# A gated-attention layer and a graph-attention layer on one core: the row of edge values turned on VectorE and carried through DRAM, and all step orders written anew

## The chip, the cores and the metric

The kernel runs on one core of a Trainium2 chip. The metric is the device time of one execution in microseconds (us), the median of several runs. Five engines work side by side on a core, each with its own instruction queue that it works off in order: TensorE (PE) multiplies, VectorE (DVE), ScalarE (ACT) and GpSimd (POOL) do elementwise work, and SyncE (SP) issues the DMAs. They wait for each other through semaphores.

## The reference

For each of 64 graphs with N = 256 nodes and H = 512 features there are two layers, each added to its input (`_layernorm` has no weights).

```
h = relu(layernorm(x))                                  # layer 0
q, k, v = h @ Wq.T, h @ Wk.T, h @ Wv.T                  # 8 heads of 64
attn = softmax(where(adj != 0, q k^T / 8, -inf))
c = attn @ v
gate = sigmoid(concat(c, h) @ Wg.T + bg)
x = x + gate * h + (1 - gate) * c

h = relu(layernorm(x))                                  # layer 1
Wh = h @ W
e_i, e_j = Wh @ a[:512], Wh @ a[512:]                   # one value per node each
e = leaky_relu(e_i[:, None] + e_j[None, :], 0.2)
p = softmax(where(adj == 0, -1e9, e), axis=2)
x = x + elu(p @ Wh)
```

## The kernel before

All arithmetic is fp32. The 256 nodes of a graph are two tiles of 128 partitions (`t` = 0, 1). The work on one graph is cut into some 215 named steps (`@step`, L358), each of which issues a few instructions on one engine. The text `PLAN` (L23) gives each step a number; L988 to L998 add 48 times the graph's number, sort all steps of all graphs by that sum and issue them in this order. The numbers serve for sorting only. The order on every engine is thus written out by hand, and steps of four or five graphs alternate. `MOVED` (L52) holds numbers of their own for graphs 0, 1, 2 and the last three, `ONCE` those of loading and preparing weights. `HOMES` says which of 8 PSUM banks (and which SBUF slot) a tile occupies; "5/7" means 5 for even graphs and 7 for odd ones. A tile put in a slot waits for the last reader of what was there before.

Each product with a weight (`qk`, `v`, `z` for the gate, `wh`) and `po` (attention times Wh) runs as seven half-size products instead of eight (`product`, L444). The seven accumulate in three PSUM tiles: tile a takes products 1 and 2, tile b takes 6, 7, 4, tile c takes 5, 3. Between them VectorE or ScalarE reads the intermediate states: `u1` reads a after 1; `u2` reads b after 6, `u3` reads b after 7, `c10` reads b after 4; `c11` reads c after 5, `c01` reads c after 3; `c00` reads a after 2. So product 7 may not start before `u2` has read b, product 4 not before `u3`, product 3 not before `c11`, product 2 not before `u1`. The operand sums that this needs (`Sh`, `Sg`, `Sc`, `S1`, `Sp`, `Rp`) are made on GpSimd (L442, L896, L906).

The other steps that matter below:

- `sc.0`, `sc.1` (L656): scores of four heads each, eight matmuls into four banks `ps`. `max` (L666, VectorE) adds the mask and takes the row maximum, two instructions for each head; `exp` (L676, ScalarE), `rec` (VectorE), `scale` (L692 GpSimd, L690 ScalarE), `turn` (L698, VectorE, 32x32 blocks), `send` and `fetch` (L554, L559, DMAs through DRAM that put the blocks in place), `we` (L716, attention times v), `cT` (L725, ScalarE), `tc` (L735), `sc_c` and `fc` (through DRAM again).
- `z.c10b`, `z.c11b`, `z.u2b` (L481, GpSimd): add the bias. `tanh` (L774, ScalarE). `diff` (L764, GpSimd): d = h - c. `plus` (L769, GpSimd): x = x + c. `mix` (L778, VectorE): d = (z + 1) d, for t = 0 and 1. `res` (L782, VectorE): x = x + d / 2. `st0`, `st1` (L506): statistics of the layer norm; `root` (L517, GpSimd), `nb` (L522), `nm` (L527, ScalarE), `th` (L535, VectorE), `sh` and `fh` (DMAs through DRAM).
- `ej` (L834): the row e_j. It is column HH of `wh[:, t, 1]`, one value per partition. For t = 0 and 1 TensorE transposes this column, broadcast to 128 columns, with the identity, so that the PSUM tile `pe` holds e_j along the free dimension on each partition. `lo` (L840, VectorE): logits from `pe`, e_i as a scalar for each partition, and the mask. `lk` (L847): leaky ReLU. `gm` (L851): row maximum. `gx` (L856, ScalarE): exponential and sums. `tg` (L867, VectorE), `sg` and `fg` (four DMAs each, L543 and L550): the turned matrix `egT`. Then `Sp`, `po`, `gr` (reciprocal), `neg`, `xn`, `pos`, `elu` (L951), `add` (L959, GpSimd), `store`.

With the numbers of `PLAN`, TensorE's repeating order from one graph's `sc.0` to the next one's is, with the graph in brackets, relative to that of `sc.0` (no bracket: the same graph):

```
sc.0 we.10(-1) we.11(-1) we.00(-1) we.01(-1) sc.1 v.7 v.5 z.1(-1) v.4 v.3 wh.1(-2) wh.6(-2) wh.5(-2) wh.7(-2)
wh.2(-2) v.2 wh.3(-2) wh.4(-2) ej(-2) z.6(-1) qk.1(+1) z.5(-1) z.7(-1) z.2(-1) z.4(-1) z.3(-1) qk.6(+1) qk.2(+1)
qk.7(+1) qk.5(+1) qk.4(+1) po.1(-2) v.6(+1) po.6(-2) po.5(-2) po.2(-2) po.7(-2) qk.3(+1) po.4(-2) po.3(-2) v.1(+1)
```

The part of VectorE's order around the reads of `qk`'s bank b, and of GpSimd's order beside it:

```
VectorE: ... z.c01(-1) mask(+1) qk.u2(+1) mix.0(-1) gr(-2) mix.1(-1) res.0(-1) res.1(-1) qk.u3(+1) st1.1(-1) ...
GpSimd:  ... diff.1(-1) z.c11b(-1) z.c10b(-1) diff.0(-1) plus.0(-1) plus.1(-1) Rp.1(-2) Rp.2(-2) Sh.3(+1) Sp.0(-2) ...
```

Of the kernel before, what the change touches and what calls it, by code (L numbers as in the profile page):

```python
# [8 lines left out]
F32 = mybir.dt.float32  # L9
# [14 lines left out]
load@-53.229 st0.0@-40.331 st0.1@-39.212 root0@-32.441 nb0@-32.4 nm0.0@-31.757 nm0.1@-31.065 th.0@-30.253  # L24
th.1@-29.213 sh@-20.792 edges@-19.41 fh@-16.267 Sh.2@-12.847 qk.1@-11.156 Sh.0@-7.731 Sh.1@-4.634 qk.u1@-4.111
qk.6@-2.798 qk.2@-1.025 mask@-0.706 qk.u2@-0.186 qk.7@0.517 qk.5@0.645 qk.u3@1.668 qk.4@1.724 Sh.3@2.277
qk.c00@2.902 v.6@6.373 qk.c11@6.599 qk.c10@7.236 qk.3@10.925 v.1@13.726 sc.0@13.916 max.000@14.395 v.u1@14.853
max.010@15.863 max.001@15.981 max.011@16.298 qk.c01@16.63 v.u2@17.05 exp.000@17.735 sc.1@17.987 exp.010@18.004
v.7@18.092 v.5@18.445 max.100@18.691 max.101@18.934 v.u3@19.508 v.c11@19.513 exp.011@20.27 max.110@20.373
max.111@21.033 exp.001@21.056 v.4@23.294 v.c10@23.754 v.3@23.804 exp.101@24.169 rec.01@24.371 v.c01@25.071  # L30
exp.111@25.413 rec.00@26.384 v.2@28.003 exp.110@28.347 rec.11@29.321 scale.111@29.428 scale.011@30.052
scale.110@30.582 turn.011@30.677 turn.111@31.368 scale.001@31.418 scale.010@31.434 scale.000@31.808
exp.100@32.801 v.c00@33.423 turn.110@37.208 send.11@37.78 rec.10@38.601 turn.001@39.658 scale.101@40.247
turn.010@40.875 turn.000@41.467 scale.100@41.474 send.00@43.588 turn.101@43.788 send.01@45.424 turn.100@45.566
send.10@52.665 fetch.11@55.316 fetch.00@56.632 Sg.0@61.755 fetch.10@62.154 fetch.01@62.554 Sg.1@62.628
we.10@63.137 we.11@63.14 we.00@63.143 we.01@63.146 cT.1@65.083 cT.0@65.432 Sc.2@65.47 Sg.2@65.68 z.1@68.201
Sc.0@68.336 Sc.1@71.528 tc.0@73.01 Sc.3@74.703 tc.1@74.778 Sg.3@82.424 z.6@83.522 z.u1@83.782 again.0@84.027
sc_c@84.628 fc@85.006 z.u2@85.037 z.u2b@86.195 z.5@86.868 z.7@86.934 z.u3@88.511 z.c11@88.533 z.2@89.652
z.4@91.004 again.1@92.033 z.c10@92.428 z.c00@92.667 z.3@93.14 diff.1@93.363 z.c11b@93.809 z.c10b@93.814
diff.0@93.855 plus.0@93.873 z.c01@93.901 tanh.11@94.368 plus.1@94.403 tanh.00@95.334 tanh.01@95.604 mix.0@96.297  # L40
tanh.10@96.664 mix.1@96.757 res.0@96.891 res.1@97.036 st1.1@99.721 st1.0@101.016 root1@101.658 nb1@104.063
nm1.1@105.297 nm1.0@107.607 th1.1@108.104 th1.0@108.66 sh1@111.487 fh1@113.781 S1.0@117.405 S1.1@117.725
wh.1@121.42 wh.6@121.622 S1.2@121.67 wh.5@121.818 wh.u1@122.472 wh.u2@122.877 wh.7@123.017 wh.2@123.434
wh.u3@124.432 wh.c11@124.598 wh.c00@125.372 S1.3@125.392 wh.3@126.07 wh.4@126.758 wh.c01@127.005 ej@127.191
wh.c10@127.609 lo.1@128.353 lo.0@129.336 lk@129.602 Rp.0@129.808 gm@131.759 gx.1@132.877 gx.0@133.43 tg@136.267
sg@136.289 Rp.1@144.203 gr@144.671 fg@145.239 Rp.2@145.991 Sp.0@148.311 Sp.1@148.553 po.1@148.676 at.0@148.676
at.1@148.686 Sp.2@149.761 po.6@152.304 po.u1@152.662 po.u2@152.749 Sp.3@153.211 po.5@153.801 po.2@154.345
po.7@154.622 po.u3@154.882 po.c11@155.143 Rp.3@155.395 po.4@156.259 po.c10@156.723 po.3@156.853 po.c00@156.874
neg.1@157.002 xn.1@157.023 po.c01@157.396 pos.1@159.011 elu.1@160.16 neg.0@163.197 add.1@163.978 pos.0@164.566
xn.0@164.664 elu.0@166.071 add.0@174.142 store.1@183.43 store.0@183.43  # L50
# [3 lines left out]
load@-69.188 st0.0@-50.682 st0.1@-46.872 nb0@-45.939 nm0.0@-43.244 nm0.1@-40.355 th.1@-36.948 Sh.0@-31.306  # L54
qk.1@-21.868 Sh.1@-15.043 Sh.2@-8.6 qk.6@-5.632 qk.u1@-5.223 qk.2@-3.198 edges@-2.003 qk.u2@-0.488 Sh.3@0.768
qk.7@2.104 qk.u3@3.685 qk.5@5.031 qk.4@7.534 qk.c11@8.518 qk.c10@8.614 mask@8.785 qk.3@9.496 qk.c00@9.714
qk.c01@10.925 sc.0@11.768 max.000@12.349 exp.000@12.811 max.011@13.719 max.010@13.827 v.1@13.828 exp.011@14.039
v.u1@15.075 v.6@16.297 max.001@16.537 v.u2@16.712 exp.010@16.947 sc.1@17.125 v.7@18.128 v.5@18.608
max.100@18.752 Sg.0@19.682 max.110@22.794 rec.01@22.94 exp.001@24.137 exp.110@24.623 max.111@24.962
scale.010@25.268 v.u3@25.413 exp.111@25.859 max.101@26.25 rec.00@26.894 scale.011@27.011 rec.11@28.365  # L60
turn.010@28.388 v.c11@28.435 scale.110@28.625 turn.011@30.554 scale.111@30.803 turn.110@31.058 scale.000@32.929
turn.111@37.156 v.2@37.693 send.01@37.944 exp.100@38.055 send.11@39.05 v.4@39.065 exp.101@39.254
scale.001@39.872 turn.000@40.017 Sg.2@40.1 v.c10@40.679 rec.10@40.871 turn.001@41.71 v.c00@42.426 v.3@43.287
scale.100@44.231 turn.100@44.288 send.00@44.4 scale.101@44.579 fetch.11@45.445 turn.101@47.476 send.10@47.487
v.c01@49.156 fetch.00@57.727 we.11@59.431 fetch.01@59.996 fetch.10@60.188 we.00@60.876 we.01@63.055 we.10@64.19
cT.0@65.308 cT.1@66.064 again.1@66.53 Sg.1@67.233 Sc.2@70.084 tc.1@71.129 Sc.0@71.252 Sc.1@72.531 z.1@73.791
tc.0@75.343 z.6@76.16 z.u1@76.575 z.5@78.53 sc_c@78.596 z.u2@79.103 z.7@81.738 Sg.3@82.04 Sc.3@82.269 z.2@84.937
fc@84.984 again.0@85.551 z.u3@85.933 z.4@86.156 z.c11@88.877 z.u2b@89.227 z.c11b@89.268 z.3@90.528 z.c10@90.685
z.c00@92.236 z.c10b@93.083 z.c01@93.161 diff.0@93.789 diff.1@95.348 tanh.10@95.709 plus.1@96.041 tanh.00@96.265
tanh.01@97.623 tanh.11@98.195 mix.1@100.765 plus.0@101.798 mix.0@102.293 res.1@102.32 res.0@102.484  # L70
st1.1@103.015 st1.0@103.627 root1@104.452 nb1@104.489 nm1.0@104.861 th1.0@105.045 nm1.1@105.996 th1.1@106.074
sh1@110.257 fh1@114.941 S1.0@118.51 S1.1@118.914 wh.1@119.88 wh.u1@121.045 wh.6@122.08 wh.u2@122.882
wh.5@123.346 wh.2@124.489 S1.2@124.759 S1.3@125.052 wh.7@126.446 wh.u3@127.178 wh.c11@127.993 wh.3@129.051
wh.4@129.297 wh.c01@129.526 wh.c10@129.674 ej@129.753 wh.c00@129.961 lo.1@130.044 Rp.0@130.295 lo.0@130.34
lk@130.611 Rp.1@131.752 gm@132.017 gx.0@132.213 gx.1@132.222 Rp.2@134.288 tg@134.329 sg@139.346 gr@146.73
fg@147.354 Sp.0@147.882 Sp.1@148.085 po.1@148.711 po.5@149.418 po.6@149.54 Rp.3@150.947 po.u1@151.6 Sp.2@151.822
po.u2@152.389 po.2@152.556 po.7@152.971 Sp.3@153.454 po.u3@154.535 po.4@155.138 po.c11@156.295 po.c10@156.812
po.3@157.112 po.c00@157.127 po.c01@157.915 neg.1@157.97 xn.1@157.979 neg.0@158.113 pos.0@158.418 pos.1@158.918
xn.0@159.242 elu.1@160.812 elu.0@162.404 add.0@162.854 add.1@165.627 store.1@179.067
""",  # L80
    1: """
load@-66.388 edges@-62.194 st0.0@-56.02 st0.1@-45.366 root0@-45.352 nb0@-40.605 nm0.0@-39.939 nm0.1@-39.434
th.1@-21.412 qk.1@-21.165 Sh.2@-20.499 Sh.0@-16.11 Sh.1@-16.042 qk.u1@-14.221 mask@-8.988 v.1@-8.931 qk.6@-3.549
v.6@-2.01 qk.u2@-1.609 v.u1@-0.158 qk.2@1.34 qk.7@2.079 qk.u3@2.277 qk.c00@3.165 Sh.3@3.954 qk.5@4.267
qk.4@5.138 v.u2@5.757 v.7@6.871 qk.c11@7.006 qk.3@7.543 qk.c10@8.787 v.u3@9.481 sc.0@11.208 max.000@12.204
qk.c01@12.588 max.010@13.45 exp.000@15.083 exp.010@15.517 max.011@15.659 exp.011@15.787 max.001@15.848
sc.1@15.867 exp.001@16.394 rec.01@17.779 max.101@19.324 max.110@19.389 scale.010@19.44 max.111@19.747
rec.00@20.491 v.2@21.238 max.100@22.063 exp.100@23.114 exp.110@23.868 v.5@24.004 scale.000@25.701 v.c11@25.88
scale.011@25.97 scale.001@26.999 v.4@27.999 turn.010@28.906 turn.000@29.132 v.c10@29.391 exp.111@30.212
turn.011@30.506 v.c00@30.783 rec.11@30.983 exp.101@32.076 scale.110@32.481 turn.001@33.017 v.3@33.133  # L90
rec.10@35.239 send.00@36.274 send.01@37.842 scale.100@38.531 scale.111@38.803 scale.101@39.584 fetch.00@39.916
# [194 lines left out]
def kernel(  # L286
# [13 lines left out]
    nc = tc.nc  # L300
    B, N, H = x.shape
    NH = 8
    DK = H // NH
    P = 128
# [528 lines left out]
    @step("ej")  # L833
    def edge_row(s, g):  # L834
        pe = s["pe"] = bank([P, N], "pe", g)
        for t in range(NT):
            nc.tensor.transpose(pe[:, t * P:(t + 1) * P], to_wh(s, g, t, 1)[:, HH:].to_broadcast([P, P]), ident)
# [193 lines left out]
```

## Time and profile before

| | |
|---|---|
| median of 3 runs | 3175.8 us (3175.29 to 3176.8) |
| profiled execution | 3175.03 us, of which the span from first to last instruction is 3173.2 |
| TensorE busy | 3097.0 us (98%), granted clock 0.997 |
| VectorE busy | 2607.4 us (82%) |
| GpSimd busy | 2176.8 us (69%) |
| ScalarE busy | 1506.8 us (47%) |
| DMA packets' share of 16 engines | 72.5%, 589.25 MB in the kernel's queue |
| `pe` transposes, TensorE | 128 matmuls, 24.4 us busy in all |

Busy time counts each instruction from start to end, and neighbours overlap in their pipelines; what an instruction costs a full queue is the distance from its start to the next one's. "Idle before" names whatever released the instruction last. Line numbers are those of the kernel before.

### The profile page before, as it was taken

To read this page: it belongs to the slowest core of one execution; us is meant where nothing else is said; L and a number is where in the kernel's file an instruction comes from. 1 tells how busy PE (TensorE), PEld (TensorE's weight loads), DVE (VectorE), ACT (ScalarE), POOL (GpSimd) and SP (SyncE) were. 2 spreads that over 40 slices of the span, in tenths; PEclk is the share of its full clock that TensorE was granted. 3 is DMA by queue.
4 is the path that set the end of the run, shared out by engine and by line. 5 is a ranking of instruction groups with operands and counts; after the bars stand their busy time and mean duration, and the time that the engine had idled before them with its cause. 6 is when DMAs were issued, how large, how long until landed. Compare 5 with 4: busy or idle time off the path is not lost.

```text
span 3173.2 us, 61830 instructions
## 1 busy us (share of the span) xinstructions
PE 3097.0 (98%) x19542; PEld 2673.1 (84%) x19542; DVE 2607.4 (82%) x6625; ACT 1506.8 (47%) x4165; POOL 2176.8 (69%) x3006
## 2 busy tenths in 40 slices
PE   9999999999999999999999999999999999999997
PEld 8888888888888888888888888888888888888885
DVE  8888888888888888888888888888888888888885
ACT  4445445455454454554544545445445454454452
POOL 4666676676766766767667667676676676766765
PEclk9999999999999999999999999999999999999998
DMA  8677776777777767777677777776776777777772
GB/s 236 166 201 179 190 204 172 195 196 180 198 177 191 204 169 196 198 178 200 177 191 203 172 196 198 177 201 176 191 204 171 196 196 177 203 176 194 194 175 81
DMA packets 1107157, 593.20 MB, mean 187 GB/s; under 512 B 687632, under 2 KB 1032720, under 8 KB 1106832
## 3 DMA queue, kind: packets, MB, share of 16 engines
q1 hardware_dynamic: 1106832, 589.25, 72.5%
q8 instruction: 157, 2.57, 0.3%
q14 instruction: 168, 1.38, 0.1%
HBM read 306.45 MB, written 282.59 MB: 186 GB/s over the span
## 4 chain that ended last, share of the span: by engine, by line
PE 78%; DVE 11%; issue 6%; DMA 5%; SPq 1%; POOL 0%; ACT 0%; DVEq 0%; POOLq 0%; ACTq 0%
PE pmb_z L457 8%; PE ps L656 8%; PE pc L716 7%; PE pmb_qk L457 6%; PE pma_z L457 5%; PE pmb_v L457 5%; PE pmb_wh L457 5%; PE pmc_z L457 5%; PE pmc_qk L457 4%; PE pma_qk L457 3%; PE pma_wh L457 3%; DMA there_e<-eb 3%; PE pma_v L457 3%; PE pmc_wh L457 3%; PE pmc_v L457 3%
## 5 line engine op out<-in xcount | busy, mean ns | idle before, releaser
L676 ACT ACTIVATE e<-e,low 128x256 f32<-128x256 f32 x1024 | 506.1, 497 | 8.8 <-DVE low L666 8.8
L666 DVE CUSTOM_DVE_ANT_0 e<-ps,mask 128x256 f32<-128x256 f32 x1024 | 379.6, 418 | 89.1 <-PE ps L656 88.1
L442 POOL TENSOR_TENSOR Sc<-cT 128x256 f32<-128x256 f32 x128 | 104.3, 815 | 506.0 <-ACT cT L725 506.0
L692 POOL TENSOR_SCALAR e<-e,rec 128x256 f32<-128x256 f32 x768 | 359.4, 485 | 18.6 <-DVE rec L683 15.4
L698 DVE STREAM_TRANSPOSE eb<-e 128x512 f32<-128x512 f32 x512 | 341.1, 688 | 0.5 <-POOL e L692 0.4
L774 ACT ACTIVATE z<-z 128x256 f32<-128x256 f32 x256 | 99.6, 412 | 405.9 <-POOL z L481 248.6
L527 ACT ACTIVATE h<-x,nb_l,rs_l 128x512 f32<-128x512 f32 x256 | 195.0, 808 | 183.3 <-DVE nb_l L522 75.8
L656 PE MATMUL ps<-qk 64*128 64x256 f32 x2048 | 255.7, 389 | 0.0
L656 PEld LDWEIGHTS ps<-qk 64*128 64x128 f32 x2048 | 187.9, 186 | 61.6 <-issue 23.2
L716 PE MATMUL pc<-eT,v 128*64 128x256 f32 x2048 | 236.7, 383 | 0.8 <-DMA eT<-there_e 0.8
L716 PEld LDWEIGHTS pc<-eT,v 128*64 128x64 f32 x2048 | 141.0, 137 | 87.9 <-issue 22.4
L676 ACT ACTIVATION_READ_ACCUMULATOR e<-e,low 128x1 f32 x1024 | 193.3, 189 | 0.0
L959 POOL TENSOR_TENSOR x<-x,po 128x512 f32<-128x512 f32 x126 | 160.3, 1272 | 32.1 <-DVE po L951 18.6
L476 ACT COPY u_po<-pma_po 128x256 f32<-128x256 f32 x63 | 23.4, 372 | 330.7 <-PE pma_po L457 321.6
L506 DVE BATCH_NORM_STATS2 bs_l<-x 128x6 f32<-128x512 f32 x256 | 172.9, 675 | 3.7 <-DMA x<-in_x_dram 3.6
L769 POOL TENSOR_TENSOR x<-x,c 128x512 f32<-128x512 f32 x128 | 172.2, 1363 | 1.5 <-DMA c<-there_c 1.1
L517 POOL TENSOR_TENSOR rs_l<-ve_l,mhalf 128x2 f32<-128x2 f32 (+1 forms) x129 | 90.4, 700 | 116.5 <-DVE ve_l L513 106.4
L535 DVE STREAM_TRANSPOSE h<-h 128x512 f32<-128x512 f32 x248 | 167.3, 694 | 0.3 <-ACT h L527 0.3
L764 POOL TENSOR_TENSOR d<-d,c 128x512 f32<-128x512 f32 x128 | 164.4, 1285 | 0.0
L778 DVE SCALAR_TENSOR_TENSOR d<-z,d 128x512 f32<-128x512 f32 x128 | 163.5, 1280 | 0.9 <-POOL x L769 0.6
L481 POOL TENSOR_TENSOR z<-z,bias 128x256 f32<-128x256 f32 x128 | 92.9, 727 | 97.2 <-DVE z L472 96.8
L782 DVE SCALAR_TENSOR_TENSOR x<-d,x 128x512 f32<-128x512 f32 x128 | 145.7, 1175 | 0.4
(175 smaller groups left out, 8953.5 us busy)
## 6 DMA issues: line engine op xcount, KB each, us to landing
there_e<-eb SPq DMA_DIRECT2D x256, 512.0 KB, 4.5
eT<-there_e SPq DMA_DIRECT2D x1024, 128.0 KB, 4.4
there_h<-h SPq DMA_DIRECT2D x496, 128.0 KB, 3.3
there_c<-cb SPq DMA_DIRECT2D x64, 512.0 KB, 3.5
c<-there_c SPq DMA_DIRECT2D x256, 128.0 KB, 2.9
x<-in_x_dram SPq DMA_DIRECT2D x63, 512.0 KB, 4.4
out_dram<-x SPq DMA_DIRECT2D x63, 512.0 KB, 3.7
hT<-there_h SPq DMA_DIRECT2D x248, 128.0 KB, 3.0
```

What stands on the lines that cost most here:

```text
L457: nc.tensor.matmul(s[name, key][(slice(None), *cols)], lhsT, rhs, start=first and i == 0, stop=last and i == len(mms) - 1, skip_group_chec ...
L506: nc.vector.bn_stats(bs, s["x"][:, t, :])
L527: nc.scalar.activation(out, s["x"][:, t, :], AF.Relu, bias=s["nb", layer][:, t:t + 1], scale=s["rs", layer][:, t:t + 1])
L535: nc.vector.transpose(h, h)
L656: nc.tensor.matmul(s["ps", half, jj, i][:, t, :], qk[r:r + DK, 0, jj, t * P:(t + 1) * P], qk[r:r + DK, 1, jj, :], start=True, stop=True,)
L666: nc.vector.tensor_tensor_reduce(e[:, i, t, :], s["ps", half, jj, i][:, t, :], s["mask"][:, t, :], -SCALE, HUGE, ALU.add, ALU.min, accum_o ...
L676: nc.scalar.activation(e, e, AF.Exp, bias=s["low", half][:, jj, i, t:t + 1], scale=-1.0, accum_out=sums[:, jj, i, t:t + 1])
L692: nc.gpsimd.tensor_scalar(e, e, rec, 1.0, ALU.mult, ALU.mult)
L698: nc.vector.transpose(eb[:, :, 4 * i:4 * i + 4, :].rearrange("p b n c -> p n b c"), e)
L716: nc.tensor.matmul(pc[i * DK:(i + 1) * DK, jj, :].rearrange("p (t a c) -> p t a c", t=NT, c=32), s["v"][:, kc, hd * DK:(hd + 1) * DK], s[" ...
L764: nc.gpsimd.tensor_tensor(d, d, s["c"][t], ALU.subtract)
L769: nc.gpsimd.tensor_tensor(xt, xt, s["c"][t], ALU.add)
```

## The change

Three things are changed. First, `ej`, for all graphs but the last two (g < LAST = 62): VectorE turns the column, broadcast to 16 columns for each t, as 32x32 blocks into a tile `turned`. Rows 0 and 16 of each block of 32 partitions then hold the block's 32 values. A new step `sj` sends them to DRAM (two DMAs of four runs of 128 bytes), a new step `fj` reads the 1 KB row back onto all 128 partitions of an SBUF tile from a new pool `row` of one buffer. `lo` is the same instruction and reads that tile in place of PSUM. Second, all of `PLAN`, `MOVED` and `ONCE` has new numbers, and so the order on each engine is another one. Third, `HOMES` is new: other banks and slots.

```
@@ -315,7 +321,7 @@
     const = pool("const", 1)
     st = pool("st", 4)
     kept = pool("kept", 5)
-    sb = {tag: pool(tag, bufs) for tag, bufs in {"x": 5, "mask": 3, "hT": 3, "wh": 1, "R": 1}.items()}
+    sb = {tag: pool(tag, bufs) for tag, bufs in {"x": 5, "mask": 3, "hT": 3, "wh": 1, "R": 1, "row": 1}.items()}
     large, medium = pool("large", 1), pool("medium", 1)
     ps = pool("ps", 1, space=bass.MemoryType.PSUM)
     dram = pool("dram", 4, space=bass.MemoryType.DRAM)
...
@@ -832,9 +838,27 @@
 
     @step("ej")
     def edge_row(s, g):
+        if g < LAST:
+            s["turned"] = small([P, 32], "turned", f"{g}")
+            e = s["wh"][:, :, 1, HH:].to_broadcast([P, NT, 16])
+            return nc.vector.transpose(s["turned"].rearrange("p (t k) -> p t k", t=NT), e)
         pe = s["pe"] = bank([P, N], "pe", g)
         for t in range(NT):
             nc.tensor.transpose(pe[:, t * P:(t + 1) * P], to_wh(s, g, t, 1)[:, HH:].to_broadcast([P, P]), ident)
+
+    @step("sj")
+    def send_row(s, g):
+        if g < LAST:
+            s["there_row"] = dram.tile([NT, 4, 32], F32, tag="row", name=f"there_row_{g}")
+            for t in range(NT):
+                rows_t = s["turned"].rearrange("(b r) c -> b r c", r=32)[:, 16 * t, :]
+                nc.sync.dma_start(s["there_row"][t], rows_t)
+
+    @step("fj")
+    def fetch_row(s, g):
+        if g < LAST:
+            s["pe"] = new("row", [P, N], "row", g)
+            nc.sync.dma_start(s["pe"], spread(s["there_row"].rearrange("t b c -> (t b c)"), N))
 
     @step("lo.0", "lo.1")
     def logits(s, g, t):
```

Of the two `PLAN` texts, the entries of the new one that stand around the steps named above (numbers for sorting only):

```
+edges@3.711 qk.3@3.892 qk.c01@4.382 qk.c00@4.567 mask@7.258 sc.0@8.025 max.001@8.607 max.010@10.017
+max.011@12.971 max.000@13.147 exp.001@14.657 exp.000@17.098 v.6@18 rec.00@19.203 v.1@19.938 exp.010@20.508
...
+wh.u3@127.396 S1.3@127.77 wh.2@128.093 wh.4@129.921 wh.c11@130.169 wh.3@130.313 wh.c01@131.348 ej@131.525
+wh.c00@132.014 wh.c10@133.179 sj@135.375 fj@137.689 lo.0@139.236 lo.1@139.363 lk@139.554 gm@139.674 gx.1@141.342
```

New homes of some PSUM tiles (even graphs/odd graphs):

```
pmb_po@7/5 ps_0_0_1@7/4 ps_0_1_0@5/7 ps_0_1_1@0 pmb_v@7/0 pma_po@4/2 pmc_po@1/4
```

Sorted by the new numbers, TensorE's repeating order is:

```
sc.0 po.1(-3) po.6(-3) v.6 po.5(-3) po.7(-3) po.2(-3) v.1 po.4(-3) po.3(-3) sc.1 z.1(-1) v.2 v.7 wh.1(-2) wh.6(-2)
wh.5(-2) wh.7(-2) v.5 wh.2(-2) wh.4(-2) wh.3(-2) z.6(-1) v.4 v.3 z.5(-1) z.7(-1) z.2(-1) z.4(-1) qk.1(+1) z.3(-1)
qk.6(+1) qk.5(+1) qk.7(+1) qk.2(+1) qk.4(+1) qk.3(+1) we.00 we.11 we.01 we.10
```

VectorE's, from `sc.0` on:

```
max.001 max.010 max.011 max.000 gr(-3) po.u2(-3) th.0(+1) tc.0(-1) rec.00 po.u3(-3) po.c11(-3) th.1(+1) po.c10(-3)
neg.1(-3) po.c01(-3) tc.1(-1) rec.01 neg.0(-3) max.111 elu.1(-3) v.u2 max.101 max.110 max.100 turn.001 wh.u2(-2)
elu.0(-3) wh.u3(-2) wh.c11(-2) turn.000 turn.011 turn.010 wh.c01(-2) ej(-2) v.u3 v.c11 rec.11 rec.10 wh.c10(-2)
v.c10 z.u2(-1) v.c01 turn.111 turn.110 z.u3(-1) turn.101 turn.100 z.c00(-1) z.c11(-1) st0.0(+2) z.c10(-1) lo.0(-2)
lo.1(-2) lk(-2) gm(-2) z.c01(-1) tg(-2) qk.u2(+1) st0.1(+2) mix.0(-1) mix.1(-1) qk.u3(+1) qk.c11(+1) res.1(-1)
res.0(-1) st1.1(-1) st1.0(-1) qk.c10(+1) nb1(-1) qk.c01(+1) th1.1(-1) nb0(+2) th1.0(-1) mask(+1)
```

Parts of GpSimd's (running on into the next round, with graphs still counted from this one) and SP's:

```
GpSimd: ... Sc.3(-1) z.u2b(-1) Sg.3(-1) Sh.3(+1) z.c10b(-1) z.c11b(-1) diff.1(-1) plus.1(-1) diff.0(-1) root0(+2)
        plus.0(-1) root1(-1) Rp.0(-2) Sg.2 Sg.0 Rp.1(-2) Rp.3(-2) Sp.0(-2) Sp.1(-2) Sg.1 Rp.2(-2) Sp.2(-2) ...
SP:     sh1(-2) fh1(-2) sh(+1) sc_c(-1) fh(+1) store(-3) send.00 send.01 sj(-2) load(+2) fc(-1) fj(-2) send.11
        fetch.01 send.10 fetch.00 fetch.11 sg(-2) fetch.10 edges(+1) fg(-2)
```

## The prediction

> **What bounds the kernel now.** I read the page's busy line first, then the TensorE timeline of two stretches, then the list of waits, then the chain of waits between 1539 and 1549 us, then the ranges of single VectorE instructions.
>
> ```profile
> PE 3097.0 (98%) x19542; PEld 2673.1 (84%) x19542; DVE 2607.4 (82%) x6625; ACT 1506.8 (47%) x4165; POOL 2176.8 (69%) x3006
> ```
>
> TensorE is the bound, and only about 2% of it is idle. The timeline shows that the work repeats in rounds, one graph further each time. One round starts with the scores of the first half (`sc.0`):
>
> ```profile
> 189.03 2.00 PE L656 MATMUL ps<-qk 64*128 64x256 f32 x16
> ...
> 236.86 2.00 PE L656 MATMUL ps<-qk 64*128 64x256 f32 x16
> ...
> 1507.09 2.00 PE L656 MATMUL ps<-qk 64*128 64x256 f32 x16
> ...
> 1555.95 2.00 PE L656 MATMUL ps<-qk 64*128 64x256 f32 x16
> ```
>
> The reader is to take differences of starts. Nearly every round lasts 1555.95 - 1507.09 = 48.86 us. The round from 189.03 lasts 47.83 us; in it TensorE shows no wait. So a wait of 1.03 us stands in the usual round. The list of waits names it, and the chain shows how it comes about:
>
> ```profile
> PE pmb_qk L457 <- DVE u_qk L472: 51.8, 62, 0.9
> ```
> ```profile
> 1539.34 1.80 PE pmb_qk L457 x16
> ...
> 1541.83 1.48 DVE d L778
> 1543.30 0.06 DVE rec L864
> 1543.36 1.00 issue
> 1544.36 0.14 DVE x L782
> 1544.50 1.00 issue
> 1545.49 1.21 DVE x L782
> 1546.70 0.61 DVE u_qk L472
> 1547.32 0.04 issue
> 1547.36 2.05 PE pmb_qk L457 x16
> ```
>
> `qk.4` may not add to PSUM bank b before VectorE has read it (`qk.u3`). Its operand was ready when `qk.7` ended, about 1544.6, but VectorE was inside the two `mix` and two `res` steps until 1546.70. Those are slow because they meet GpSimd:
>
> ```profile
> L778 DVE SCALAR_TENSOR_TENSOR d<-z,d x128: 677/1150/1746, 80.2 to 3136.6; 128x512 f32<-128x512 f32 x128
> L782 DVE SCALAR_TENSOR_TENSOR x<-d,x x128: 677/1209/1575, 82.0 to 3139.1; 128x512 f32<-128x512 f32 x128
> ```
>
> The same instruction takes 677 ns at best and about 1200 in the median.
>
> [...] The transfers that repeat every round here land in 2.9 to 4.5 us (medians) and are far larger[...]. [...]
>
> **The change part by part.** All sums are per round, with time 0 at `sc.0`.
>
> *Transposes removed.* In the timeline the two `pe` transposes start at 1526.81 and the next step at 1527.03: 0.22 us, wholly on TensorE's path. A round without any wait becomes 47.83 - 0.22 = 47.61 us.
>
> *Row sent instead.* `ej` on VectorE: 32 columns; reciprocals of 4 columns take 156 ns, a transpose of 512 takes 688, so 0.15 to 0.2 us. `sj` adds two DMA issues and `fj` one to SP: issues with 128 rows or blocks cost 0.43 (`eT`) to 0.8 us, so 0.9 to 2.4 us of queue, and I take 1.5. `lo` now reads two SBUF operands instead of one in PSUM: 0.48 us each now, at worst 2 x 0.5 us longer when GpSimd is met, at best a little shorter. None of this is on TensorE's path if the row lands in time. In the new order `ej` comes after `wh.c01`, about 20 us; `sj` is issued by 21.5 and lands by 24 to 26; load and four fetches (0.47 + 1.74) stand before `fj`, so SP waits at most some 2 us there; the row lands by 27 to 30. `lo` stands behind `z.c10`, whose product ends at about 30. Cost: nothing, as long as that holds; a later row would hold VectorE, and behind it `lk`, `gm`, `tg` and `qk.u2`, for which TensorE waits.
>
> *The u_qk wait.* Laying the new TensorE order end to end with the start-to-start times of the timeline (`sc` 1.93, `po` 0.43, `v` and `wh` 0.87, `z` 1.73, `qk` 1.79, `we` 0.90) puts `qk.6` at 32.9, `qk.5` 34.7, `qk.7` 36.5, `qk.2` 38.3, `qk.4` 40.05. `qk.u3` can start at 38.5 and must start by 39.3. Ahead of it on VectorE now stand only `qk.u2` (34.9 to 35.6), `st0.1` (0.8) and two `mix`; the two `res` come after it. `mix` waits for `diff.0`: GpSimd starts `z.c10b` at about 30.4, then 0.7 + 0.7 + 3 x 1.27 = 35.6. So `mix.0` starts at 36.5 and meets `plus.0` (1.2 us), `mix.1` does not (0.6): 38.3. `qk.u3` is in time with 0.8 us to spare, and the 1.03 us go.
>
> *What is late next.* At the start of the round the new order puts `po.1`, `po.6`, `v.6`, `po.5`, `po.7` right after `sc.0`, where four `we` stood. The homes give `pmb_po` of one parity the bank of `ps_0_1_0` of the other. So `po.6`, due at 2.46 (1.93 + 0.43 + 0.1 that TensorE loses when it changes from scores to other products), waits for `max.010`. In the trace the first max starts 1.16 us after `sc.0`, and each takes 0.69: `max.001` 1.16 to 1.85, `max.010` from 2.0, read by 2.8. That is 0.35 to 0.4 us. Then `po.7` needs `po.u2`, which stands behind `max.011`, `max.000` and `gr` (2.75 + 0.69 + 0.69 + 0.1 = 4.2, read by 4.6); TensorE comes there at 2.85 + 0.43 + 0.87 + 0.43 = 4.58: about even. In rounds of the other parity `v.6` needs `max.011`'s bank (3.5 against 3.3). After a wait TensorE loses another 0.1 (1.00 us instead of 0.89 for the first eight matmuls after 1547.36). Together 0.45 to 0.75 us, and I take 0.6.
>
> *Round and total.* 47.61 + 0.6 = 48.21, against 48.86: 0.65 us less. 58 rounds follow the repeating order and six have orders of their own with smaller waits of the same kind; I count 60: 39 us. The profiled execution took 3175.03 us (span 3173.2 and 1.8 around it); the median of the runs, 3175.8, is 0.8 above it. So 3175.8 - 39 = 3137. The first and last graphs are reordered too; the trace can't price that, and I allow 6 us either way.
>
> **Rivals.**
> - *No new wait*: the maxes start earlier than I think, or the banks come free. For it: TensorE now waits nearly nowhere else. Against: two maxes are 1.4 us of VectorE after scores that take 1.9. Round 47.61, 1.25 x 60 = 75 less: 3101.
> - *The old wait is replaced in full*: GpSimd runs 1 to 2 us later than laid out, `mix.0` meets more, `qk.u3` is late again, on top of the wait at `po.6`. For it: GpSimd's list is long just there. Against: 0.8 us to spare and two `res` moved away. Round 48.5 to 48.95: 3155 to 3181, and I name 3165.
> - *Slower: the second layer's chain sets the round.* `lo` to `po.1` took 1527.61 to 1549.25 = 21.6 us; in the new order 30.3 to 50.1 (`po.1` of the next round), 19.8, with an SP queue of 55 DMAs instead of 52 between. Laid out: `gm` ends 32.4, `gx` 34.0, `tg` 34.7, four sends 3.25, `fetch.10` (4 x 0.6) and `edges` 0.4 go before `fg` (3.3), last landing 4.2 after its issue: 48. TensorE's first `po.1` waits for that landing at 50.1, so 2.1 us are spare. A delay of the row, of `tg` or of SP beyond 2.1 + 0.65 = 2.75 us makes the kernel slower; at 3.4 us the round is 49.5 and the time 3175.8 + 0.65 x 60 = 3215. For it: SP is in order, `sg` waits for VectorE, and landings of `eT` reach 6.6 us. Against: three independent steps would have to slip.
>
> That the change doesn't do what it says is possible only for the spreading apart: one of four `mix` and `res` still meets GpSimd in my layout, which the sum contains.
>
> **How the numbers follow.** Forecast 3137 (its own range 3120 to 3153): 0.52. No new wait: 0.17. Old wait replaced in full: 0.20, of which a third lies within 0.2% (6.4 us, about what can be told from no change here). Slower chain: 0.11. Faster by over 0.2%: 0.52 + 0.17 + 0.14 = 0.83; within: 0.06; slower: 0.11. The range from 3094 to 3176 leaves out the slower chain, the top of the third case and the bottom of the second.
>
> **What would show it.** Right: `pe` gone from TensorE; the wait of `pmb_qk` for `u_qk` near 0; new waits of 0.3 to 0.5 us of `pmb_po` (and `pmb_v` in every second round) for the max steps; `mix` and `res` with medians under 0.9 us except one; a round of 48.1 to 48.4. Wrong: `pma_po` waiting for the landing of `egT`, `eg` (`lo`) waiting for the row's DMA, a `pc` wait for `eT`, or `pmb_qk` still waiting about 1 us. Any wait at another step of TensorE above 0.3 us a round breaks the sum.

## The result, and the profile after

The changed kernel takes 3173.3 us (median of 12 runs, 3167.5 to 3182.5), the kernel before 3176.9 (12 runs on the same chip, 3175.3 to 3178.0). The ratio is 0.9989, with a 95% interval of 0.998 to 0.9999. The forecast was 3137. So 3.6 us were gained where 39 were expected. Also the runs now lie 15 us apart where they lay 3 us apart. The profiled execution of the changed kernel took 3169.5 us (span 3167.6, clock 0.997).

The busy line of the changed kernel:

```profile
PE 3106.2 (98%) x19418; PEld 2656.4 (84%) x19418; DVE 2579.7 (81%) x6687; ACT 1484.6 (47%) x4165; POOL 2182.6 (69%) x3006
```

TensorE has 124 matmuls fewer (62 graphs of two transposes), yet it is as full as before. The waits of TensorE over the whole span (what was waited for; total us, times, longest):

```profile
PE pmb_po L463 <- POOL Sp L920: 20.0, 57, 2.8
PE pmb_qk L463 <- DVE u_qk L478: 9.9, 13, 2.7
PE pc L722 <- DVE qk L478: 4.4, 28, 0.2
PE pc L722 <- DMA eT<-there_e: 4.3, 2, 2.7
```

The wait of 51.8 us in 62 pieces for `u_qk` is gone except for 13 pieces. Two groups are new, one in nearly every round (`pmb_po`) and one in every second round (`pc`). The ranges of `mix` and `res` (minimum, median, maximum in ns) are now those of undisturbed instructions:

```profile
L784 DVE SCALAR_TENSOR_TENSOR d<-z,d x128: 650/691/1759, 78.4 to 3131.5; 128x512 f32<-128x512 f32 x128
```
```profile
L788 DVE SCALAR_TENSOR_TENSOR x<-d,x x128: 659/684/1302, 80.7 to 3133.2; 128x512 f32<-128x512 f32 x128
```

They had medians of 1150 and 1209. So both things that the change is made of did happen. The timeline of TensorE shows where the rest went. It holds the starts of three rounds and the steps around the new waits (start, duration, step; in brackets the idle time and what ended it):

```profile
1503.40 2.00 PE L662 MATMUL ps<-qk 64*128 64x256 f32 x16
...
1506.35 0.67 PE L463 MATMUL pmb_po<-Rp,Sp 128*128 128x256 f32 x2 [0.24 <-POOL Sp L920]
1506.95 1.13 PE L463 MATMUL pmb_v<-wv_t,Sh 128*128 128x256 f32 x4
1507.91 0.59 PE L463 MATMUL pmc_po<-wh,Sp 128*128 128x256 f32 x2
...
1548.17 1.08 PE L722 MATMUL pc<-eT,v 128*64 128x256 f32 x8
1549.41 2.81 PE L722 MATMUL pc<-eT,v 128*64 128x256 f32 x24 [0.16 <-DVE qk L478]
1552.15 2.00 PE L662 MATMUL ps<-qk 64*128 64x256 f32 x16
...
1555.11 0.67 PE L463 MATMUL pmb_po<-Rp,Sp 128*128 128x256 f32 x2 [0.33 <-POOL Sp L920]
1555.61 1.03 PE L463 MATMUL pmb_v<-wv_t,Sh 128*128 128x256 f32 x4
1556.47 0.59 PE L463 MATMUL pmc_po<-wh,Sp 128*128 128x256 f32 x2
...
1596.80 3.67 PE L722 MATMUL pc<-eT,v 128*64 128x256 f32 x32
1600.40 2.00 PE L662 MATMUL ps<-qk 64*128 64x256 f32 x16
```

Rounds now alternate: 1552.15 - 1503.40 = 48.75, and 1600.40 - 1552.15 = 48.25. At 1555.11 `po.6` waits 0.33, as forecast. The profile names GpSimd's `Sp` as the releaser. But the sum that `po.6` reads, `Sp.1`, had ended at 1553.2; it is `max.010`, whose second instruction ended at 1554.95, that sets the bank free. (In the last experiment below all four `Sp` of a round end before `max.010` does, and `po.6` still starts 2.95 us into the round.)

In rounds like the one from 1503.40, `v.6` has the bank of `max.011`, which ended at 1506.88: it starts at 1506.95, 0.60 after `po.6` where the other round has 0.50, and `pmc_po` comes 0.96 after it instead of 0.86. The forecast had this too; the list of waits doesn't show it, since the matmuls before it hadn't ended.

The new thing is 1549.41. The four `we` groups of an odd graph take 1552.15 - 1548.17 = 3.98 us, those of an even one 1600.40 - 1596.80 = 3.60. In between, `we.11` waits for the bank of `pc_1`, which in that parity is the bank of `pmc_qk` that `qk.c01` still reads. That is 0.38 in every second round.

A third thing happens in some rounds only. First SP's queue in one of them, then VectorE, then TensorE:

```profile
1818.20 2.02 SPq L565 DMA_DIRECT2D c<-there_c  x4
1820.35 0.35 SPq L861 DMA_DIRECT2D row<-there_row  x1
```
```profile
1826.84 2.35 DVE L866 SCALAR_TENSOR_TENSOR eg<-row,wh,mask 128x256 f32<-128x256 f32 x2 [0.84 <-DMA row<-there_row]
1829.22 1.64 DVE L872 SCALAR_TENSOR_TENSOR eg<-eg 128x512 f32<-128x512 f32 x1
```
```profile
1834.08 1.16 PE L463 MATMUL pmb_qk<-Sh,wq_t 128*128 128x128 f32 x8 [1.46 <-DVE u_qk L478]
```

The row is fetched behind four fetches of `c`, and by the start of `lo` it lands 6.5 us after its issue (1820.35 to 1826.84; the DMA packets' share in between was 1.11). `lo` waits 0.84 for it. Started late, the two `lo` and `lk` meet GpSimd's `diff` and `plus` (1827.45 to 1830.31): they take 2.35 us and 1.64; in an undisturbed round they take 1.35 and 1.10. So `gm`, `tg` and then `qk.u2` are late, and `qk.7` stands 1.46 us. That round lasts 50.48. The fetch is not a small transfer, either. It writes the 1 KB row onto 128 partitions:

```profile
row<-there_row SPq DMA_DIRECT2D x1, 128.0 KB
```

That is as much as one fetch of `eT` moves.

From the starts of the scores I worked out where the span stands against that of before:

```
stretch                              before    after    difference
to the first scores                    24.0     24.2      +0.2
first six rounds                      261.7    263.7      +2.0
the 54 repeating rounds              2639.2   2628.0     -11.1
the last rounds and the tail          248.3    251.7      +3.4
```

In the 54 rounds, 48.21 a round was forecast, 2603.3 in all. The 24.7 above it are, but for rounding, 27 x 0.38 = 10.3 at `we.11`, 8.8 in ten rounds longer than 48.25 or 48.76, and 27 x 0.04 + 27 x 0.17 = 5.7, since a round with nothing but the waits at `po.6` and `v.6` is 48.25 or 48.38 (seen below) and not 48.21.

### The profile page after: what moved, and what is told of

It is laid out like the page before. It is cut to its first block, busy times and chain, and to the rows that moved or that the text cites. A ratio compares the mean times of both kernels' runs of the same rounds, so it can differ in the third digit from the quotient of the medians.

```text
span 3167.6 us, 61736 instructions
## 1 busy us (share of the span) xinstructions
PE 3106.2 (98%) x19418; PEld 2656.4 (84%) x19418; DVE 2579.7 (81%) x6687; ACT 1484.6 (47%) x4165; POOL 2182.6 (69%) x3006
## 5 line engine op out<-in xcount | busy, mean ns | idle before, releaser
L698 POOL TENSOR_SCALAR e<-e,rec 128x256 f32<-128x256 f32 x768 | 405.7, 541 | 327.0 <-DVE rec L689 253.2
L523 POOL TENSOR_TENSOR rs_l<-ve_l,mhalf 128x2 f32<-128x2 f32 (+1 forms) x129 | 113.4, 879 | 320.6 <-DVE ve_l L519 312.3
L704 DVE STREAM_TRANSPOSE eb<-e 128x512 f32<-128x512 f32 x512 | 332.2, 686 | 1.3 <-POOL e L698 1.3
L482 ACT COPY u_qk<-pma_qk 128x512 f32<-128x512 f32 x64 | 37.5, 585 | 459.0 <-PE pma_qk L463 459.0
L487 POOL TENSOR_TENSOR z<-z,bias 128x256 f32<-128x256 f32 x128 | 107.9, 862 | 157.8 <-DVE z L478 157.8
L696 ACT ACTIVATE e<-e,rec 128x256 f32<-128x256 f32 x256 | 116.0, 504 | 207.9 <-DVE rec L689 207.9
L770 POOL TENSOR_TENSOR d<-d,c 128x512 f32<-128x512 f32 x128 | 187.9, 1468 | 1.6 <-ACT d L533 1.6
L482 ACT COPY qk<-pma_qk 128x512 f32<-128x512 f32 x64 | 37.5, 586 | 278.6 <-PE pma_qk L463 273.2
L463 PE MATMUL pmb_qk<-Sh,wq_t 128*128 128x128 f32 x1024 | 136.4, 276 | 8.9 <-DVE u_qk L478 8.9
L478 DVE TENSOR_TENSOR u_z<-pmb_z,u_z 128x256 f32<-128x256 f32 x128 | 53.7, 420 | 110.8 <-PE pmb_z L463 110.6
```

The source lines that it names most:

```text
L463: nc.tensor.matmul(s[name, key][(slice(None), *cols)], lhsT, rhs, start=first and i == 0, stop=last and i == len(mms) - 1, skip_group_chec ...
L698: nc.gpsimd.tensor_scalar(e, e, rec, 1.0, ALU.mult, ALU.mult)
L704: nc.vector.transpose(eb[:, :, 4 * i:4 * i + 4, :].rearrange("p b n c -> p n b c"), e)
L770: nc.gpsimd.tensor_tensor(d, d, s["c"][t], ALU.subtract)
```

## Experiments

The theory after the result: the wait for `u_qk` did go, and three things took its place or came with it: the bank at `po.6` (A1, forecast), the bank at `we.11` (A2), and the row's late landing (B). Rivals: that the wait is only handed on within the same chain of VectorE, whatever the change; and that the way through DRAM is free after all. The edits change places in the written order, and two of them the way the row takes. Where an edit is shown, only the words that change are printed.

### One move in the kernel before

```diff
-qk.u3@1.668
+qk.u3@0.8
```

> The kernel before, with one place in its order changed: qk.u3 stands on VectorE ahead of res.0 and res.1 of the graph before instead of behind them. Nothing else of the change is in it. My theory (the wait of 1.03 us a round at qk.4 was only for qk.u3 behind mix and res): the wait goes, rounds fall from 48.86 to about 47.8, so about 3176 - 57 = 3115 to 3125 us, which would beat both kernels. Rival (the old wait is only handed on, to po.1's start for egT or to the first matmuls of the next stage, because res comes later now): rounds of 48.4 to 48.9, 3150 to 3180 us.

Measured: 3158.2 us (3157.5 to 3160.3), ratio 0.9946 (0.9933 to 0.9958). The waits of TensorE:

```profile
PE pmb_po L457 <- DVE u_po L472: 22.9, 55, 0.7
PE pmc_po L457 <- DVE qk L472: 5.8, 28, 1.0
...
PE pmb_qk L457 <- DVE u_qk L472: 2.7, 5, 1.0
```

Neither the theory nor the rival was right in full. The wait for `u_qk` is gone (2.7 instead of 51.8), though `mix` still has a median of 1148 ns and `res` of 828. So the place behind `res` made that wait, more than the slow instructions as such. But the rounds are 48.53 and not 47.8: of 1.03 us, 0.70 came back at `po`. On VectorE, `res` now runs later:

```profile
1586.16 1.51 DVE L782 SCALAR_TENSOR_TENSOR x<-d,x 128x512 f32<-128x512 f32 x2
...
1590.72 0.68 DVE L506 BATCH_NORM_STATS2 bs_l<-x 128x6 f32<-128x512 f32 x1
...
1591.77 0.41 DVE L472 TENSOR_TENSOR u_po<-pmb_po,u_po 128x256 f32<-128x256 f32 x1
```

`po.u2` at 1591.77 stands behind the norm's statistics of a graph that is needed only much later, and `po.7` waits 0.64 for it, in every second round; in the others `pmc_po` waits 0.18 and `po.7` 0.19. This one move alone gains 18 us, five times what the change gained.

### The same, with the norm behind po

```diff
-st1.0@101.016 root1@101.658 st0.0@-40.331 qk.u3@1.668
+st1.0@102.61 root1@102.62 st0.0@-39.24 qk.u3@0.8
```

> The kernel before with qk.u3 ahead of res (as in b1) and, on VectorE, the statistics of the next norm moved back: st1.0 behind qk.c11, st0.0 behind po.u2. Theory (in b1 the gain of 1.03 a round came to 0.33 only because res, later now, pushed qk.c11 and po.u2 late, for which pmc_po and po.7 waited 0.34 to 0.80 a round): those waits go, rounds of 47.8 to 48.0, 3158 - 35 = about 3120 to 3130 us. Rival (the later norm hands it on again: hT or h1T late, a stage further): rounds of 48.3 or more, 3145 to 3160.

Measured: 3149.4 us (3149.2 to 3150.1), ratio 0.9916 (0.9903 to 0.993). Rounds are 48.12 and 48.58. The rival was nearer: of the 35 us expected, 8.7 came. `po.7` waits 0.23 in every second round, and in the others `pmc_po` still waits 0.18 for `qk.c11` and `sc.0` now waits 0.25 for ScalarE's `po.c00`. The waits move along the chain of `po`, each time smaller.

### we.01 ahead of we.11

```diff
-we.01@53.108
+we.01@53.104
```

> The changed kernel with we.01 ahead of we.11 on TensorE, nothing else. Theory A (half of the rounds of the changed kernel are 48.76 and not 48.25 because we.11 of an odd graph needs the PSUM bank that qk.c01 of the next graph has not read yet): the matmul group between gives qk.c01 time, all usual rounds become about 48.25, 29 x 0.5 = 14 us less than the changed kernel, about 3155 to 3160. Rival (the wait only moves to the group that is now first, or the odd rounds are long for another cause): rounds still alternate, 3167 to 3173.

Measured: 3164.4 us (3162.7 to 3167.5), ratio 0.9966 (0.9953 to 0.9978), 8.9 below the changed kernel's median. The wait of `pc` for `qk` is gone. The rounds that took 48.76 take 48.38. So A2 holds for 0.38 of the 0.51; the rest is the start of these rounds, above all `v.6` at the bank of `max.011`. Its profile happens to be rich in late rows (`lo` waits 13 times, 9.7 us), and has the longest of all repeating rounds. TensorE after that wait, and granted clock and DMA share over three stretches of 6 us (columns: stretch, length, busy us and count of PE, PEld, DVE, ACT, POOL, then the clock, DMA share, GB/s):

```profile
1933.57 1.30 PE L463 MATMUL pmb_qk<-Sh,wq_t 128*128 128x128 f32 x8 [2.70 <-DVE u_qk L478]
1934.67 1.92 PE L463 MATMUL pmb_qk<-Sh,wk_t 128*128 128x128 f32 x8
...
1937.98 1.06 PE L463 MATMUL pma_qk<-hT,wk_sb 128*128 128x128 f32 x8
```
```profile
1926.00:1932.00 6.00, 4.88 (x39) 4.53 (x37) 5.33 (x5) 1.81 (x5) 3.80 (x3) 1.00 1.08 270
1932.00:1938.00 6.00, 4.43 (x25) 4.43 (x26) 4.79 (x10) 1.42 (x6) 2.32 (x2) 0.72 0.53 99
1938.00:1944.00 6.00, 6.00 (x56) 5.45 (x56) 5.48 (x13) 2.09 (x3) 1.53 (x3) 1.00 0.50 138
```

The row was fetched at 1919.14, behind the coefficients, and `lo` started at 1925.80. TensorE stood 2.70 us and ran eight matmuls in 1.10 (after the wait of 1.46 above they took 1.00), then eight in 214 ns each and eight more in 200, instead of 111; the granted clock over 1932 to 1938 was 0.72. The round lasted 52.97 instead of 48.38: 2.70 of wait, some 0.16 of restart, and 1.7 of slow matmuls. A wait of this length doesn't always do it: one of 2.75 at 228 us cost nothing beyond itself in the changed kernel (clock 1.00 over 224 to 236, round 51.58), and 1.6 us more in a later run, that with both moves (clock 0.86 over 224 to 236, round 53.20). In the profile of this experiment the wait at that place was 3.22, and the round took 54.84. After the three waits of 1.45 and 1.46 in the changed kernel's repeating rounds the clock was 1.00 (over 1832 to 1838, 1931 to 1937 and 2612 to 2618). What makes the difference after waits of 2.70 and 2.75 was not shown.

### The row's fetch ahead of the coefficients

```diff
-fc@88.684
+fc@89.8
```

> The changed kernel with the fetch of the row issued on SyncE ahead of the four fetches of the second coefficients instead of behind them. Theory B (late rows make the sporadic long rounds): the row lands 1 to 2 us earlier, lo doesn't wait for it, the rounds of 49.3 and 50.5 go, 3160 to 3165 us, and the runs lie within 4 us of each other. Rival (lo and lk are late because they share SBUF with GpSimd, or the fetch is slow whenever it is issued): the rounds stay, 3168 to 3180.

Measured: 3163.8 us (3161.3 to 3169.1), ratio 0.9965 (0.9951 to 0.9978), 9.5 below the changed kernel. The waits of `lo` in its profile:

```profile
DVE eg L866 <- DMA row<-there_row: 2.7, 2, 1.7
```

They were ten, of 7.8 us. In the 54 rounds one is longer than it should be, by 0.3; the sum of the 54 is 2619.5 where 27 x 48.25 + 27 x 48.76 is 2619.3. B holds for these rounds. The row is now issued at about 23.9 in the round and not at 25.2; whether the earlier start or the shorter queue before it is what helps, this run doesn't tell apart. The runs still lie 8 us apart, not within 4.

### Both moves

> The changed kernel with both single moves together: we.01 ahead of we.11 on TensorE, and the fetch of the row ahead of the second coefficients on SyncE. If the two costs are separate (a bank in every second round, a late row in some rounds), the gains add: rounds of 48.25 and 48.38, no long rounds, 3173 - 9 - 9.5 = about 3152 to 3157 us, about 0.65% below before. If they are one cause seen twice: 3161 to 3165, as each alone.

Measured: 3151.2 us (3150.5 to 3156.6), ratio 0.9925 (0.9912 to 0.9939), 22.2 below the changed kernel. The two gains add, and a little more (8.9 + 9.5 = 18.4). The 54 rounds are 48.25 and 48.38 without exception but two (0.1 to 0.24 longer). These are two costs and not one.

### The row by TensorE again

```diff
+    def sent(g):
+        return g in (0, 1, 2, LAST - 1)
-        if g < LAST:
+        if sent(g):
-ej@131.525
+ej@135.2
```

The condition is changed in `ej`, `sj` and `fj`; the other graphs take the branch with the two transposes, into bank 1 or 6.

> The changed kernel with the row of edge values of graphs 3 to 57 made by TensorE transposes into PSUM again, as before; all else of the change stays (the orders, the VectorE steps). Theory B (the row's late landing, and lo and lk reading SBUF beside GpSimd, make the sporadic rounds of 49.3 and 50.5 and the spread of the runs): the pair of lo is near 0.95 us again, no such rounds, +0.22 a round for the transposes: rounds of 48.45 and 48.95, so 3169 + 12 - 10 = about 3165 to 3175 with a spread under 4 us. Rival (the row through DRAM costs nothing, the long rounds have another cause): 3180 to 3185, with the long rounds still there.

Measured: 3177.0 us (13 runs, 3172.8 to 3181.9), ratio 1.0003 (0.9995 to 1.0011). The repeating rounds are 48.47 and 48.98, exactly 0.22 more than the changed kernel's, and none of them is as long as 49.3. The range of `lo`:

```profile
L870 DVE SCALAR_TENSOR_TENSOR eg<-pe,wh,mask x120: 473/475/484, 268.2 to 3154.0; 128x256 f32<-128x256 f32 x120
```

It is 475 ns with one operand in PSUM, with a maximum of 484; with both in SBUF, in the changed kernel, the minimum is 473, the median 945 and the maximum 2299. The SBUF operand as such costs nothing at best; the 71 of 124 that took 0.7 us or more all ran beside GpSimd instructions, for over nine tenths of their time. In the kernel before, with one operand in PSUM, 126 of 128 did so too, and none took more than 485. So the row's way through DRAM brought 3.7 us as it stands (3177.0 to 3173.3; the two intervals overlap, so this is not clear of the noise) and 13.2 once the row is fetched first (3163.8). But the runs of this kernel lie 9 us apart without any row from DRAM (but for those of the first three graphs and one of the last). So late rows can't be all of the spread.

### Both in another execution

> The changed kernel unchanged, a second look: its runs go from 3167.5 to 3182.5 us and its profile was of 3169.5. Theory B (late rows make the difference between its runs): the span differs from the first look by the rounds that are longer than 48.25 and 48.76, and each of them has lo waiting for the row, with 1.5 us of wait before qk.7, or 2.7 and then slower matmuls. Rival: long rounds without a late row.

> The changed kernel with the row by TensorE transposes, unchanged, a second look: its runs went from 3172.8 to 3181.9 us though no row comes late in it. If something else than the row spreads the runs, its long rounds show it (a fetch of the attention matrix that lands late, the first graphs): a span 3 to 8 us above the first look's 3171.9 with those rounds named. If the span is again 3171 to 3174, the cause of that spread stays open.

Measured: the changed kernel 3165.0 us, span 3163.2. In the 54 rounds, late ones add 4.3 us in this execution and 8.8 in the first (`lo` is late in all of them but one, which is 0.05 longer); `lo` waits for the row nine times (4.7 us) and ten times (7.8). Taken off, both come to about 3161. So late rows do make the difference between these two executions. The kernel with the row by TensorE took 3174.4, with the same rounds as before (one longer, by 0.15). What carries its other runs up to 3181.9 wasn't caught in a profile and stays open.

### Cover for po.6

```diff
+        if 4 <= g <= 57:
+            own.update({"we.01": 53.104, "we.10": 56.1, "cT.1": 62.9})
```

with `fc@89.8`. One `we` group (0.9 us) goes between `sc.0` and `po.1`.

> As the run with both moves, and for graphs 4 to 57 one group of we (we.10) put behind sc.0 as cover for po.6, which waits there for the bank that max.010 reads (cT.1 goes behind it on ScalarE). Theory (the bank shared by pmb_po and ps_0_1_0 costs 0.35 to 0.45 a round, as the forecast's fourth step had it): that wait goes, rounds of 47.8 to 48.0, 20 us below the run with both moves, about 3130 to 3138. Rival (cT.1 and the coefficients come late, or another bank takes the wait's place): rounds of 48.2 or more, 3150 to 3160.

Measured: 3155.4 us (3154.7 to 3159.9), ratio 0.9939 (0.9926 to 0.9951), 4.3 slower than without the cover. Rounds are 47.78 and 48.96. In the first kind no wait is left at `po`: the same rounds took 48.38 without the cover, so the banks at `po.6` and `v.6` cost 0.60 there with all that goes with them. In the other, `po.6` doesn't wait either, but `po.7` does. The two engines there:

```profile
1546.20 0.57 ACT L731 COPY cT<-pc 128x512 f32<-128x512 f32 x1
1546.67 0.38 ACT L482 COPY u_po<-pma_po 128x256 f32<-128x256 f32 x1
```
```profile
1547.65 0.67 PE L463 MATMUL pmb_po<-Rp,Sp 128*128 128x256 f32 x2 [0.67 <-POOL Sc L448]
```

`po.u1` on ScalarE came behind `cT.1`, which I had moved; VectorE's `po.u2` behind it ended at 1547.50, and that, not GpSimd's `Sc`, released `po.7`.

### Three more orders with the cover

```diff
-    own.update({"we.01": 53.104, "we.10": 56.1, "cT.1": 62.9})
+    own.update({"we.01": 53.104, "we.10": 56.1, "cT.1": 62.9, "po.u1": 158.65})
```

and the rows of graphs 1 and 2 fetched early (`fj@134.9`, `fj@136.5`, and `fc` of graph 2 at 87.0).

> The run with the cover for po.6, with two things mended: for graphs 4 to 57 po.u1 stands ahead of cT.1 on ScalarE (in the run with the cover every second round lost 0.83 at po.7, for u_po, which came behind cT.1), and the rows of graphs 1 and 2 are fetched ahead of the coefficients too (the wait of 2.75 at 228 us). Theory (po.6's bank wait of the changed kernel is worth 0.35 to 0.6 a round, and nothing else holds TensorE there): rounds of about 47.8 in both parities, 3155 - 29 x 1.15 - 4 = about 3115 to 3125 us, below every kernel so far. Rival (the other parity has another wait behind that one, or exp is late for the shift): rounds of 48.3 or more remain, 3135 to 3150.

Measured: 3190.9 us (3189.9 to 3192.8), ratio 1.0045 (1.0031 to 1.0058). The theory fell. Rounds are 49.02 and 49.08, and its waits say why:

```profile
PE pmb_po L463 <- DVE u_po L478: 26.4, 30, 1.1
PE pmc_po L463 <- issue: 17.6, 26, 0.7
```

In one parity `pmc_po` waits up to 0.7 for the bank of `pc_1`, which `cT.1` reads; `cT.1` now starts 1.27 us after `po.u1`. In the other the last `pmb_po` waits up to 1.1 for VectorE.

> The same with the row of graphs 3 to 57 made by TensorE transposes into PSUM again. It prices the row's way where nothing else is late. Theory (the forecast's first two steps were right once the row lands in time: two transposes are 0.22 a round, the way through DRAM is free): 0.22 a round more, 55 x 0.22 = 12 us above the run it is compared with. Rival (the row's way through DRAM costs VectorE and the queue something even then): less than 6 us above, or below it.

The edit is that of the run with the row by TensorE, on top of this. Measured: 3205.3 us (3201.7 to 3206.8), ratio 1.0089 (1.0075 to 1.0103), 14.4 above. Rounds are 49.24 and 49.30: 0.22 more, as the theory said. The two transposes cost 0.22 a round in two different orders, and the row through DRAM nothing in the rounds where it lands in time.

```diff
-    ... "cT.1": 62.9, "po.u1": 158.65})
+    ... "cT.1": 62.6, "po.u1": 158.64})
```

with `we.01`, `we.10` as above, and of the early rows only that of graph 2.

> The cover for po.6 again (we.10 behind sc.0 for graphs 4 to 57, with we.01 first and the row ahead of the coefficients), now with cT.1 and then po.u1 ahead of exp.001 on ScalarE, and the row of graph 2 fetched early. In the last try cT.1 stood behind po.u1 and exp.001, and po.5 waited for the bank of pc_1 that cT.1 reads. Theory (ScalarE's order was what took back the cover's gain): neither po.6, po.5 nor po.7 waits over 0.3, rounds of 47.8 to 48.1 in both parities, 3120 to 3135 us. Rival (exp.001, now about 1 us later, or another reader takes its place: TensorE's work at po is so close to its inputs that any shift meets the next): rounds of 48.3 to 49, 3150 to 3190.

Measured: 3174.9 us (13 runs, 3171.9 to 3178.1), ratio 0.9996 (0.9988 to 1.0004). Rounds are 48.55 and 48.96; `pmb_po` waits for `u_po` in 57 pieces of 34.4 us. The rival holds. The wait at `po.6` is real, but a cover there doesn't pay: `po.u2` and `po.u3` need VectorE, which is full of the maxima just then, and the next step of `po` waits instead.

### The row of graph 2, and GpSimd beside res

> The run with both single moves (we.01 first, row ahead of the coefficients) and the row of graph 2 fetched ahead of the coefficients as well, which its own order had left behind them. Theory (a late row costs its wait and then TensorE's slower rate after an idle stretch of nearly 3 us): the wait of 2.75 before qk.7 at about 228 us goes, the round there falls from 53.2 to about 49, all else stays: 3151 - 4 = 3146 to 3148 us. Rival (the wait there has another cause, lo beside GpSimd or the norm of the first layers): 3150 to 3153.

The edit, on top of both moves, is `fj@138.629` to `fj@136.5` for graph 2. Measured: 3151.7 us (3149.7 to 3154.1), ratio 0.9924 (0.9911 to 0.9936). The wait of 2.75 is gone and its round falls from 53.20 to 49.69, but the first six rounds together only from 264.5 to 262.7, since the round from 85 us on was 2.5 longer in this execution. The medians don't differ. Inconclusive for the time.

```diff
-Rp.0@149.174 Rp.1@152.539 Rp.3@153.048
+Rp.0@144.1 Rp.1@144.15 Rp.3@144.2
```

> The run with both single moves (we.01 first, row ahead of the coefficients; 3151 us), with three of GpSimd's sums for po (Rp.0, Rp.1, Rp.3) moved ahead of the norm's root, so that they run where res.0 and res.1 run on VectorE; in the changed kernel GpSimd is idle there. Theory C (that mix and res stand apart from GpSimd is needed: their own time sets when qk.c11, qk.c10 and then the scores' maxima come): the pair of res goes from 1.28 to about 2.0 to 2.5 us, the norm and qk.c10 come 0.7 to 1.2 later, rounds grow by 0.3 to 1.0: 3170 to 3210 us. Rival (res is off the path now that qk.u3 stands ahead of it: VectorE waits 0.2 to 0.3 behind it for other engines anyway): rounds of 48.25 and 48.38 as before, 3148 to 3156.

Measured, on top of both moves: 3152.9 us (3150.9 to 3155.2), ratio 0.9928 (0.9914 to 0.9942). The range of `res` in it, and without the edit:

```profile
L788 DVE SCALAR_TENSOR_TENSOR x<-d,x x128: 657/1124/1230, 80.2 to 3114.7; 128x512 f32<-128x512 f32 x128
```
```profile
L788 DVE SCALAR_TENSOR_TENSOR x<-d,x x128: 657/682/1306, 80.9 to 3115.9; 128x512 f32<-128x512 f32 x128
```

`res` takes 1124 ns again, and the usual rounds are still 48.25 and 48.39. Four others of the 54 are 0.3 to 1.1 us longer; in two of them `wh` waits for GpSimd's `S1`, and whether the moved sums delay it is open. Theory C fell, the rival holds: once `qk.u3` stands ahead of `res`, the usual round doesn't get longer when `res` meets GpSimd. For `mix` this wasn't tried.

## Why the prediction was wrong

*Transposes removed, 0.22 a round*: right, to the hundredth, in two orders.

*The u_qk wait goes, 1.03 a round*: right for the repeating rounds, but for those with a late row. The reason was half right: the place of `qk.u3` decides (one move in the kernel before removes the wait with `mix` at 1148 ns), and in the order with both moves the keeping apart of `res` pays nothing of its own.

*What is late next, 0.45 to 0.75, taken as 0.6*: right in kind and nearly in size. `po.6` waits 0.24 to 0.33 for `max.010`'s bank (forecast 0.35 to 0.4), and `v.6` for that of `max.011` in every second round, as forecast; `po.7`, "about even", doesn't wait. With the other costs taken away, rounds are 48.25 and 48.38 against 48.21: 5.7 us over the 54.

*The sum of waits*: this step failed. "Any wait at another step of TensorE above 0.3 us a round breaks the sum" named the danger. I had compared banks only at the start of the round. `we.11` at its end waits for the bank that `qk.c01` reads, 0.38 in every second round: 10.3 us in the profile, 8.9 in the medians of the run that took it away.

*The row sent instead, "Cost: nothing, as long as that holds"*: this failed in some rounds. The row was to land by 27 to 30 in the round, which was my estimate; the fetch behind four others was issued at 25.4, took 6.5 us and landed at 31.9. So the landing was mis-sized: the prediction took the fetch for far smaller than the transfers whose medians of 2.9 to 4.5 us it gave, by the row's 1 KB in DRAM. But it moves 128 KB like a fetch of `eT`, whose landings the prediction itself had noted to reach 6.6. That its size makes the landing late was not tested. The order of costs, `lk`, `gm`, `tg` and `qk.u2`, was right. I had priced `lo`'s two SBUF operands as beside TensorE's path; with a late row they are on it: a wait of 0.84 became 1.46 at TensorE, and one of 1.55 became 2.70, with 1.7 of slow matmuls on top (granted clock 0.72 over 6 us). 8.8 and 4.3 us in two executions, 9.5 in the medians.

*First and last graphs, ±6*: I had counted 0.65 of gain in six more rounds, 3.9 us. Measured were 0.20 + 1.96 + 3.36 = 5.5 lost, 9.4 away from that. TensorE's waits account for it: 6.5 us in the first six rounds against 3.8 before (2.75 of them behind the late row of graph 2), and 17.7 against 14.8 in the last rounds and the tail. What makes these waits was followed at that one place only and stays open.

Together 10.3 + 8.8 + 5.7 + 9.4 = 34.2; the profiled spans differ by 5.6 where 39 was forecast, which is 33.4 (the 0.8 is that 54 rounds from 48.87 in the mean to 48.21 are 35.8, not 54 x 0.65 = 35.1, and rounding). The median is another 3.8 above the profiled execution. Late rows may be part of the cause, but that is only argued: there is no profile of those runs, and the kernel without late rows spreads by 9 us too.

*The rivals*: "the old wait is replaced in full" gave 3165, nearest to what came, but by another mechanism: `mix.0` and `qk.u3` are in time.

## What to carry to other kernels

When a wait of the bounding engine is taken away, lay the whole next round over every resource, each bank with its last reader in both parities, and not only the steps beside the change. A short chain that goes through memory needs its issue placed early, ahead of the other fetches on its queue: here that was worth 9.5 us, more than the whole change. And a fetch that spreads a row over 128 partitions isn't small: this one moved 128 KB. Before an order is made anew, try the one move that the wait names; here it was worth 18 us, and with two like it 27.

## What the runs showed of the hardware

After TensorE had stood for 2.70 us in one execution, it ran eight matmuls in 1.10 us and the next sixteen in 214 and 200 ns instead of 111, with a granted clock of 0.72 over 6 us. After a wait of 2.7 us at another place the clock was 0.86 over 12 us in one execution, and after one of 2.75 there it was 1.00 in another. A VectorE instruction of 128x256 took 475 ns with one operand in PSUM; with both in SBUF it took 473 at best and 945 in the median, up to 2299 beside GpSimd. A row of 1 KB fetched onto 128 partitions by one DMA was there 6.5 us after its issue in one late round, with a DMA share of 1.11 in between.
